# GpSimd's queue for the stores of staged weight sums, and a shorter lead for side work

## The chip, the cores and the metric

The kernel runs on one core of a Trainium2 chip. The metric is the device time of one execution in microseconds, the median of several runs. A core has a matrix engine (TensorE, PE in the profile), a vector engine (VectorE, DVE), a scalar engine (ScalarE, ACT), a general engine (GpSimd, POOL) and a sync engine (SyncE, SP) that here only issues transfers. Each engine has one queue of instructions and works through it in order. An instruction that waits for a semaphore holds everything behind it in its queue. SP, ACT and POOL can issue transfers; 16 DMA engines carry them out.

## The reference

All data is float32. For each of 4 batches there are 2048 tokens of width 512 and a context of 128 rows. The block does a gated cross attention and then a gated expert layer:

```python
Q = layernorm(x) @ Wq + bq;  K = ctx @ Wk + bk;  V = ctx @ Wv + bv
attn = softmax(Q @ K.T) / sqrt(512)
x = x + tanh(g_xattn) * (attn @ V)
z = layernorm(x)
e = argmax(z.mean(over tokens) @ Wr + br)          # one of 8 experts for a whole batch
h = relu(z @ W1[e] + b1[e])                        # 512 -> 2048
x = x + tanh(g_ffn) * (h @ W2[e] + b2[e])          # 2048 -> 512
```

Which expert a batch uses is known only once all its tokens have been through attention.

## The kernel before, in words

The two products of the expert layer are most of the arithmetic. The kernel computes them with Strassen's scheme in the Winograd form, which needs seven products of half-size blocks instead of eight, and for the first layer it does so on two levels. The price is sums and differences of blocks: of the weights, of the tokens z, and of the products. In the code a product is one of seven numbers, and `ORDER` gives their order.

The weights' sums are made once for each batch and half of the hidden width (`fh`), and this is called staging. `stage_half` loads a tile `base` with a part of W1 (`base_load`, line 593), forms sums in it and in a tile `tt` with `minus` (line 564), and stores both to the scratch arrays W1d in DRAM. It also loads a part of W2 into a tile named `base2` (`base2_load`, line 599), forms sums in place (`second_sums`) and stores that to W2d. Under the products GpSimd makes these sums. There is one buffer for `base` and one shared by `tt` and `base2`, so each load waits until the store of what lay there has landed. All stores go through `put` (line 584), which also tells the planner that the data will be there 9 us later. The first batch's weights are partly staged before the products begin, in tiles called `home` that are later used for other things.

The product loop takes weight tiles from a ring: four of one kind and two of the other. `fetch` issues the loads of these tiles on SP (lines 777, 784 and 790) as soon as a place is promised free, and an instruction on SP waits until TensorE has finished with the tile that lay there. `z_load` (line 888), the loads of y (957), the loads of xT (207) and the output stores (1137) are on SP too.

In a first-layer pass (`ffn1`) VectorE and GpSimd combine the seven products with running sums r and u. GpSimd makes those of lines 1000, 1006 and 1011. VectorE's line 1063 writes such a sum into the PSUM bank that the next product adds to, so TensorE waits for it. Second-layer passes (`ffn2`) have no work of that kind on GpSimd. There are 16 passes of each sort.

The order on every queue is written out by a planner in the kernel's own Python, at build time. It keeps a clock that a product loop advances (`tick`). Attention of later batches (the stream `slow`) and staging (`staged`) are generators that yield estimates of their steps' times; after each tick, `paced` lets them take steps, as their share allows and as long as the step's estimated start is no more than `SOON[0]` ahead of the clock (1.4 us before). `SOON` is also the size of a deliberate gap (`GAP`) after some steps of attention: after the power on GpSimd that gives rstd (line 220), after the exponentials, and after the copy of their transpose. Before the products begin, streams run by another rule, and the flag `ahead_of_ffn` tells the two apart.

The planner counts GpSimd's sums in `free["POOL"]`; a store takes no time there. `land` moves keys to the set `made` when the 9 us are over, and `fetch` only issues loads of weights that are in it.

Of the kernel before, what the change touches and what calls it, by code (L numbers as in the profile page):

```python
# [89 lines left out]
def flamingo(tc, ctx, x, xT, cxT, g_x, g_f, WqT, Wk, Wv, bqk, bv, Wr, br, W1, b1, W2, b2, out):  # L90
    nc = tc.nc
# [68 lines left out]

    zsum, Zs = {}, {}

    SOON = [1.4]
    MV = {}
    done_at, clock = {}, {"now": 0.0}
    ahead_of_ffn, fetched = [True], [0, 0]
# [9 lines left out]
    def room(ps):  # L176
        while held[ps] == ROOM[ps]:
            yield (("DMA", 0.3),)
        held[ps] += 1
# [16 lines left out]
    def attention(b, blk, pools):  # L196
# [13 lines left out]
        def statistics():  # L210
# [9 lines left out]
            nc.gpsimd.tensor_tensor(rstd, ve, mhalf, ALU.pow)  # L220
            yield ("DVE", 0.15), ("POOL", 1.05), ("GAP", 0.0 if ahead_of_ffn[0] else SOON[0])
            return mv, rstd
# [29 lines left out]
        for t in range(4):  # L252
# [4 lines left out]
            if t % 2:  # L257
                yield ("ACT", 1.2), ("GAP", SOON[0] * (t // 2) * (not ahead_of_ffn[0]))
        yield from room(ps_t)
# [9 lines left out]
        nc.vector.tensor_scalar(coef, coef, gx, None, ALU.mult)  # L269
        yield (("ACT", 0.6), ("GAP", SOON[0] * 0.8 * (not ahead_of_ffn[0]))), (("DVE", 0.4),)  # L270
        while MV[b][1] is None:
# [309 lines left out]
    made, landing = set(), []  # L581
    LAND = 9.0

    def put(dst, src, *keys):
        nc.sync.dma_start(dst, src)
        landing.append((clock["now"] + LAND, keys))

    def land(by):
# [14 lines left out]
    def second_sums(b, fh, kp, t, eng):  # L603

        b11, b21, b22, b12 = (t[:, i] for i in range(4))
        for o, l, r in ((b11, b12, b11), (b12, b22, b12), (b22, b22, b11), (b21, b21, b22)):
            yield minus(eng, o, l, r)
        put(
            W2d[b, fh][:, kp].rearrange("p o k c -> p o (k c)"), t,
            *((b, fh, "2") for _ in range(kp))  # L610
        )

    def first_half():
# [11 lines left out]
        def keep(place, n, pc, t):  # L625

            d, o = W1d[0, 0, place]
            put(d[:, o : o + n, pc], t, *((0, 0, place + j) for j in range(n * pc)))
# [53 lines left out]
    def stage_half(b, fh, eng, turns):  # L682
# [12 lines left out]
        def first_layer(pc, base):  # L695
            yield from inner_sums(eng, base)
            if pc and turns:
                yield (("DMA", 4),)
            tt = stp.tile([P, 3, 7, P], F32, tag="tt", name="tt")
            for i, took in enumerate(  # L700
                outer_sums(eng, *(t[:, i] for t, n in ((base, 4), (tt, 3)) for i in range(n)))
            ):
                yield took
                if i == 2:
                    put(W1d[b, fh, 4][0][:, :, pc], tt, *((b, fh, 4 + j) for j in range(3 * pc)))
            put(W1d[b, fh, 0][0][:, :, pc], base, *((b, fh, j) for j in range(4 * pc)))
# [620 lines left out]
    def paced(name, stream, more):  # L1327

        due[name] = min(due[name] + more, 1.0 + more)
        while stream and due[name] >= 1 and stream.at <= clock["now"] + SOON[0]:  # L1330
            due[name] -= 1
# [4 lines left out]
    def tick(dt, weight):  # L1336
# [5 lines left out]
        for s_ in list(loose):  # L1342
            while s_.at <= clock["now"] + SOON[0]:
                if not s_.step():
# [61 lines left out]
```

## Time and profile before

| | |
|---|---|
| median of 3 runs | 1742.46 us (1736.89 to 1744.96) |
| profiled execution, its own time | 1742.86 us |
| its span | 1741.1 us |
| TensorE busy, share of the span | 1686.3 us, 97% |
| VectorE, ScalarE, GpSimd busy | 1048.7, 581.9, 654.6 us |
| mean granted clock of TensorE | 0.989 of full speed |
| HBM traffic | 262.99 MB read, 117.44 MB written |

The page of a profile gives busy times, a row for each kind of instruction and for each kind of transfer. A wait is shown as who waited, at which line, for whom. SP's queue has waits of its own (SPq): they are no work, but they hold what stands behind. In a list by stretch of time, each pair of numbers is the busy time of an engine and its instructions in that stretch, and the granted clock of TensorE follows, as a share of full speed. Staging under the products lies at about 130 to 280, 420 to 635, 750 to 970 and 1080 to 1270 us.

### The profile page before, as it was taken

To read this page: it belongs to the slowest core of one execution; us is meant where nothing else is said; L and a number is where in the kernel's file an instruction comes from. 1 tells how busy PE (TensorE), PEld (TensorE's weight loads), DVE (VectorE), ACT (ScalarE), POOL (GpSimd) and SP (SyncE) were. 2 spreads that over 40 slices of the span, in tenths; PEclk is the share of its full clock that TensorE was granted. 3 is DMA by queue.
4 is the path that set the end of the run, shared out by engine and by line. 5 is a ranking of instruction groups with operands and counts; after the bars stand their busy time and mean duration, and the time that the engine had idled before them with its cause. 6 is when DMAs were issued, how large, how long until landed. Compare 5 with 4: busy or idle time off the path is not lost.

```text
span 1741.1 us, 21919 instructions
## 1 busy us (share of the span) xinstructions
PE 1686.3 (97%) x7965; PEld 1439.3 (83%) x7966; DVE 1048.7 (60%) x1663; ACT 581.9 (33%) x1284; POOL 654.6 (38%) x536
## 2 busy tenths in 40 slices
PE   6889999999999999998999999999999999999999
PEld 5667788888888888787878788888888888888887
DVE  5756576556666674757648565583846464746362
ACT  1524225253251614514144252322323242414150
POOL 0365424420648621366156520576514210331010
PEclk8989999999999999999999999999999999999999
DMA  7267777465687965478769564679744543545242
GB/s 296 97 255 287 280 259 287 157 237 190 247 324 259 356 235 178 156 284 299 288 244 344 193 229 142 228 276 318 292 150 155 164 160 101 180 145 174 91 136 80
DMA packets 143067, 381.87 MB, mean 219 GB/s; under 512 B 10480, under 2 KB 40176, under 8 KB 128624
## 3 DMA queue, kind: packets, MB, share of 16 engines
q1 hardware_dynamic: 136912, 342.43, 55.9%
q10 hardware_dynamic: 6048, 38.04, 5.5%
q8 instruction: 64, 1.05, 0.2%
q14 instruction: 43, 0.35, 0.1%
HBM read 262.99 MB, written 117.44 MB: 219 GB/s over the span
## 4 chain that ended last, share of the span: by engine, by line
PE 86%; DVE 6%; DMA 4%; issue 1%; ACT 1%; POOL 1%; SPq 0%; DVEq 0%; POOLq 0%; ACTq 0%
PE Y L811 34%; PE Q L811 23%; PE X L811 21%; DMA w<-W1d 3%; PE pav L288 2%; PE psc L234 2%; PE pt L335 1%; DVE st L214 1%; DMA home<-in_W_dram 1%; PE pm L417 1%; PE pv L450 1%; DVE x L276 1%; DVE c L1009 1%; PE pk L417 0%; DMA wq<-in_WqT_dram 0%
## 5 line engine op out<-in xcount | busy, mean ns | idle before, releaser
L811 PE MATMUL Y<-z,w 128*128 128x256 f32 x1296 | 322.8, 382 | 18.0 <-DMA w<-W1d 8.8
L811 PEld LDWEIGHTS Y<-z,w 128*128 128x128 f32 x1296 | 242.7, 190 | 65.2 <-DVE Q L1063 12.8
L978 ACT ACTIVATE h<-c,b1T 128x256 f32<-128x256 f32 x512 | 229.5, 500 | 86.8 <-DVE c L1009 37.1
L564 POOL TENSOR_TENSOR base<-base 128x512 f32<-128x512 f32 (+1 forms) x126 | 183.5, 1462 | 175.5 <-DMA base<-in_W_dram 171.2
L830 ACT COPY Y<-X 128x512 f32<-128x512 f32 x144 | 82.2, 571 | 467.6 <-PE X L811 467.2
L811 PE MATMUL Y<-w,h 128*128 128x256 f32 x1024 | 228.8, 380 | 0.0
L811 PE MATMUL X<-w,h 128*128 128x256 f32 x1024 | 227.9, 379 | 0.0
L811 PE MATMUL Q<-w,h 128*128 128x256 f32 x1024 | 226.9, 379 | 0.0
L811 PEld LDWEIGHTS X<-w,h 128*128 128x128 f32 x1024 | 193.9, 190 | 29.0 <-issue 3.1
L811 PEld LDWEIGHTS Y<-w,h 128*128 128x128 f32 x1024 | 194.7, 191 | 28.1 <-issue 2.0
L811 PEld LDWEIGHTS Q<-w,h 128*128 128x128 f32 x1024 | 194.3, 190 | 26.2
L811 PE MATMUL Q<-z,w 128*128 128x256 f32 x864 | 212.1, 385 | 1.3
L811 PE MATMUL X<-z,w 128*128 128x256 f32 x864 | 207.4, 379 | 0.0
L811 PEld LDWEIGHTS Q<-z,w 128*128 128x128 f32 x864 | 164.8, 193 | 28.6 <-issue 4.2
L1000 POOL TENSOR_TENSOR r<-r,cg 128x512 f32<-128x512 f32 x32 | 40.6, 1270 | 390.3 <-DVE cg L1081 388.4
L811 PEld LDWEIGHTS X<-z,w 128*128 128x128 f32 x864 | 163.5, 190 | 24.8 <-issue 3.3
L564 POOL TENSOR_TENSOR z<-z 128x256 f32<-128x256 f32 x156 | 129.0, 851 | 37.4 <-DVE z L564 33.6
L220 POOL TENSOR_TENSOR rstd<-ve,mhalf 128x4 f32<-128x4 f32 x32 | 34.9, 1089 | 279.1 <-DVE ve L219 279.0
L811 PE MATMUL Y<-w,s 128*128 128x256 f32 x512 | 113.6, 379 | 0.0
L1142 DVE SCALAR_TENSOR_TENSOR y<-Y,gf,y 128x512 f32<-128x512 f32 x64 | 47.8, 746 | 103.1 <-PE Y L811 101.9
L811 PEld LDWEIGHTS Y<-w,s 128*128 128x128 f32 x512 | 96.8, 190 | 12.9
L1142 DVE SCALAR_TENSOR_TENSOR y<-X,gf,y 128x512 f32<-128x512 f32 x32 | 23.9, 746 | 135.3 <-issue 70.7
(145 smaller groups left out, 2081.9 us busy)
## 6 DMA issues: line engine op xcount, KB each, us to landing
w<-W1d SPq DMA_DIRECT2D x108, 512.0 KB, 4.3
w<-W1d SPq DMA_DIRECT2D x108, 384.0 KB, 4.4
w<-W2d SPq DMA_DIRECT2D x64, 512.0 KB, 7.2
base<-in_W_dram SPq DMA_DIRECT2D x29, 1024.0 KB, 8.5
W1d<-base SPq DMA_DIRECT2D x14, 1792.0 KB, 9.3
w<-in_W_dram SPq DMA_DIRECT2D x48, 512.0 KB, 5.1
W1d<-tt SPq DMA_DIRECT2D x14, 1344.0 KB, 6.0
xT<-in_xT_dram SPq DMA_DIRECT2D x16, 1024.0 KB, 10.9
```

Of the source, the lines that this page charges most:

```text
L214: nc.vector.bn_stats(st, xt[:, t, :])
L220: nc.gpsimd.tensor_tensor(rstd, ve, mhalf, ALU.pow)
L234: nc.tensor.matmul(psc[:, t, :], lhsT=xTt[:, kc, t * P : (t + 1) * P], rhs=Mb[:, kc, :], start=kc == 0, stop=kc == KC - 1,)
L276: nc.vector.scalar_tensor_tensor(xt[:, t, :], t_, coef[:, t : t + 1], xt[:, t, :], ALU.mult, ALU.add)
L288: nc.tensor.matmul(pav[t][0], lhsT=pT[:, t * P : (t + 1) * P], rhs=Vb, start=True, stop=True)
L335: nc.tensor.transpose(pt[kc][0][:, t * P : (t + 1) * P], z[:, t, kc * P : (kc + 1) * P], ident)
L564: eng.tensor_tensor(o, l, r, ALU.subtract)
L811: nc.tensor.matmul(bank[:, c, :], lhsT=left(k, c), rhs=right(k, c), start=fresh and c == 0 and k == 0, stop=c == 1 and k == ks - 1, skip_g ...
L830: nc.scalar.copy(t["Y"], t["X"])
L978: nc.scalar.activation(h[ij][:, v, 2 * m + c, :], src[:, c, :], AF.Relu, bias=b1T[:, f + c : f + c + 1],)
L1000: eng.tensor_tensor(r[j], r[j], v, ALU.add)
L1142: nc.vector.scalar_tensor_tensor(o, v, gf, o, ALU.mult, ALU.add)
```

## The change

`put` issues its transfer on GpSimd's queue when the products have begun (`ahead_of_ffn` is then false), and on SP's queue before that, as it did. `SOON` becomes 0.8. Since the planner uses `SOON`, the order of attention and staging among the products changes on every queue, while the amount of work stays.

```diff
-    SOON = [1.4]
+    SOON = [0.8]
...
+    def staging_queue():
+        return nc.sync if ahead_of_ffn[0] else nc.gpsimd
+
     def put(dst, src, *keys):
-        nc.sync.dma_start(dst, src)
+        staging_queue().dma_start(dst, src)
         landing.append((clock["now"] + LAND, keys))
```

## The prediction

> **What bounds the kernel now.** I read the page first, for who is busy.
>
> ```profile
> span 1741.1 us, 21919 instructions
> PE 1686.3 (97%) x7965; PEld 1439.3 (83%) x7966; DVE 1048.7 (60%) x1663; ACT 581.9 (33%) x1284; POOL 654.6 (38%) x536
> w<-W1d SPq DMA_DIRECT2D x108, 384.0 KB, 4.4
> W1d<-base SPq DMA_DIRECT2D x14, 1792.0 KB, 9.3
> ```
>
> TensorE is busy 97% of the span, and the change neither adds nor removes a product, so a gain can only come out of its pauses. The two transfer rows matter later: a weight tile normally lands 4.4 us after its issue, a store of staged sums takes 9.3.
>
> Second, busy time by stretch (columns: start:end, length, then busy us and instructions of PE, PEld, DVE, ACT, POOL; granted clock, DMA share, GB/s). The cuts are where staging starts and stops.
>
> ```profile
> 130.00:280.00 150.00, 143.15 (x678) 121.83 (x677) 96.02 (x155) 56.96 (x128) 65.30 (x45) 0.98 0.74 274
> 280.00:420.00 140.00, 138.42 (x668) 117.36 (x667) 86.15 (x156) 54.74 (x125) 33.66 (x38) 1.00 0.56 198
> 420.00:635.00 215.00, 213.01 (x1027) 181.39 (x1026) 138.44 (x222) 73.73 (x168) 123.11 (x93) 1.00 0.82 298
> 750.00:970.00 220.00, 209.39 (x995) 177.48 (x994) 140.79 (x215) 73.37 (x167) 117.45 (x87) 0.99 0.77 283
> 1080.00:1270.00 190.00, 188.78 (x870) 164.29 (x869) 122.34 (x140) 57.10 (x116) 121.54 (x88) 1.00 0.77 269
> 1270.00:1730.00 460.00, 459.51 (x2124) 402.30 (x2123) 242.74 (x341) 143.61 (x290) 92.61 (x86) 1.00 0.43 140
> ```
>
> The four stretches with staging hold 6.9 + 2.0 + 10.6 + 1.2 = 20.7 us of TensorE's pauses; the 460 us without staging hold 0.5. Third, the list of waits says for what (total us, times, longest).
>
> ```profile
> PE Y L811 <- DMA w<-W1d: 8.8, 5, 3.6
> PE Y L811 <- DVE Q L1063: 7.4, 7, 2.8
> POOL base L564 <- DMA base<-in_W_dram: 171.2, 14, 27.6
> ```
>
> Fourth, the waits of SP's own queue from 130 to 1300 us.
>
> ```profile
> SPq L585 <- POOL base L564: 67.6, 21, 10.2
> SPq L585 <- POOL tt L564: 43.5, 11, 10.2
> SPq L585 <- POOL home L564: 11.0, 1, 11.0
> SPq L599 <- DMA W1d<-tt: 11.7, 7, 3.7
> SPq L593 <- DMA W1d<-base: 8.5, 4, 4.9
> ```
>
> SP, which must issue every weight tile in order, stands 122.1 us at the stores' line (585) until GpSimd has made the sums, and only 20.2 us at the later loads that reuse the stored tile. Fifth, the chain of waits shows what such a stop can cost (start, us, what), and two windows of 10 us give the clock.
>
> ```profile
> 163.73 1.74 POOL home L564
> 165.48 0.33 SPq L585
> ...
> 167.35 9.11 DMA w<-W1d
> ...
> 176.59 1.57 PE Y L811 x4
> ```
> ```profile
> 170.00:180.00 10.00, 6.43 (x25) 5.19 (x24) 5.05 (x8) 5.16 (x16) 9.77 (x6) 0.84 1.02 386
> 810.00:820.00 10.00, 7.78 (x28) 5.89 (x27) 8.34 (x15) 6.06 (x14) 8.80 (x6) 0.83 1.03 408
> ```
>
> The sum ends, the store leaves, only then two loads of y and a weight tile go out, all at once (386 GB/s); the tile takes 9.11 us instead of 4.4 and TensorE stood 3.57 us. After it the clock is 0.84 over 10 us: another 1.6 us.
>
> **The change, part by part.** It moves 45 of the 54 stores (14 of 1792 KB and one of 896 KB from base, 14 of 1344 KB from tt, 16 of 1024 KB into W2d) from SP's queue to POOL's; the nine issued before the products stay. It also lowers SOON from 1.4 to 0.8, which reorders attention and staging against the products. The profiled execution took 1742.86 us outside its span of 1741.1, beside the median of 1742.46, so the sum below is as good against either.
>
> *1. SP no longer stops at stores.* Behind them stand weight tiles (lines 777 to 790), y, xT and z loads. The stall at 173 to 176.6 us should go: y and the tile can be issued before 165, while the DMA is less loaded. Gain 3.57 + 1.6 = 5.2. The other weight waits are 8.8 - 3.6 = 5.2. One of 2.1 follows the two stores of 776.8 and 778.8 us: the tiles behind them left at 779.4 and took 9.9 us to land. I take that whole, and half of the remaining 3.1, since there base loads of 1 MB stand in front as well, which stay on SP: 2.1 + 1.6 = 3.7. Ends: 0 and 10.4 us for the two together; I take 8.9.
>
> *2. The new order.* In the program's order, between the first and last running sum that POOL makes of a first-layer pass (lines 1000, 1006, 1011), there stand 35 staging sums before the change and 10 after it, plus 6 stores. The first pass keeps its 4. These sums delay POOL's running sums and slow VectorE's own: line 1009 takes 0.69 us, up to 1.94 where POOL works beside it. VectorE's L1063 is then late and TensorE waits. Past the first pass that wait is 7.4 - 2.8 = 4.6 us, and the window at 810 adds 0.17 x 10 = 1.7 by its clock: 6.3. From 31 to 6 + 6 intruders, the loss falls by 19/31: gain 3.9 (ends 0 and 6.3).
>
> SOON itself removes no work. Every planner step comes up to 0.6 us later, so attention's last block ends after 2028 of 3360 product calls instead of 1834, and staging after 2520 instead of 2282. That costs nothing as long as the pieces keep ahead of their use: the last batch's first half is stored by call 2286 and used from 2520, the second half's first-layer sums by 2448 and used from 2730. If that lead were gone, the planner would issue staging in one piece with TensorE idle behind sums of some 5 us; the margin excludes it. TensorE's stalls on attention (pav on L276 3.1 us, with a clock of 0.95 after it) are dealt anew: 0, ends -4 and +8.
>
> *3. POOL pays.* No row shows a DMA issued by POOL. Lower end: SP's issue of the same stores, 0.33 to 0.56 us. Upper end: POOL held until the data landed, 7.5 us (median of these stores). I take 1.5: the smallest POOL instruction with its fixed cost (L220, 1.02 us) plus about SP's 0.5 for writing the pieces; it lies near the lower end because the work is the same as SP's. 45 x 1.5 = 68 us raise POOL from 655 to 722 us of 1741, still idle most of the time. It counts only where something waits for POOL: 8 stores stand directly ahead of a running sum and 7 ahead of rstd (L220), behind which VectorE's line 241 and all after it wait. SOON leaves 0.8 us of slack; of the remaining 0.7 us I let half reach TensorE (the PSUM banks cover some): 15 x 0.35 = 5.2. With 0.5 us for a store it is 0; with 5 us, 15 x 4.2 / 2 = 31. The store waits only for POOL's sums just before it, so the wait itself adds nothing to POOL's queue.
>
> *4. The wait that is next.* The loads at 593 and 599 need the store landed. SP reaches them sooner, since it is not held at 585, and the store leaves about 1 us later: the 20.2 us there will grow, I estimate to 40 to 60, and POOL's wait for base loads (171.2) with it. Weight tiles behind them were issued already or go out as late as now: 1 us (ends 0, 8).
>
> Sum: -5.2 - 3.7 - 3.9 + 5.2 + 1 = -6.6; 1742.9 - 6.6 = 1736 us.
>
> The Trainium skill, in "DMA: Bandwidth & Descriptors" (Issuing engines are not separate DMA queues), speaks against a gain: all issuers feed the same 16 engines, and another issuer saves only sequencer time. The measured 9.11 and 9.9 us against 4.4 include being queued behind other transfers, so the rule does not settle it; by it item 1's tiles would land as late as now, and the result would be near 1745. The same page's section Queues, rings and completion order has each engine alternate between queues by packets, which would let a tile pass a 1792 KB store; no run here shows it. The page puts the first byte of a DMA from GpSimd at about 1 us against 0.6, so a store would leave some 0.4 us later; by that price alone item 3 would cost 0.
>
> **Rivals.** *A, slower: POOL held by its stores.* If writing the pieces of a store (four rows per partition) takes GpSimd 4 us, item 3 is 15 x 3.2 / 2 = 24, and the result 1742.9 - 12.8 + 24 + 1 = 1755. It decides from the length at which 15 x (d - 0.8) / 2 eats 11.8 us: d = 2.4 us. For it: the base wait of 171.2 us shows that staging is tight, and POOL's queue is in order; against: POOL idles 62%. *B, all pauses go:* 10.4 + 6.3, pav's 4, nothing paid: about 1722. For it: 31 sums leave the first-layer passes; against: the DMA share is 1.02 in the stalled windows, whoever issues. *C, hidden anyway:* the tiles stay late because bandwidth is the limit, and POOL's cost cancels the new order's gain: 1742. *D, it does not do what it says:* excluded, the order shows 45 stores on POOL and no other change of work.
>
> **How the numbers follow.** Main forecast 0.47 (1736, own range 1728 to 1743, which is d from 0.5 to 2.4 us), A 0.30, B 0.13, C 0.10. The bound that a measurement can tell is 0.5%, 8.7 us, so 1733.8 and 1751.2. Faster: B and 0.23 of the main case, 0.36. Slower: A from d = 3.5 us on, 0.26. Same: the rest, 0.38. Range: from 1724, near B, to 1757, past A's 4 us.
>
> **What would show it.** SP's waits at 585 under the products gone and those at 593 and 599 at 40 to 60; TensorE's wait on w<-W1d under 3 us; its wait on L1063 near 5; POOL's stores at 1.5 us or less each. Wrong if POOL's stores take over 2.4 us, if VectorE's line 241 waits on rstd for many microseconds, or if tiles land as late as before.

## The result, and the profile after

The changed kernel takes 1758.16 us (1756.99 to 1763.36) beside 1742.93 us of the kernel before on the same chip: a ratio of 1.0101, interval 1.0079 to 1.0123. It is slower by 15 us; the forecast was 1736 (1724 to 1757). The profiled execution took 1757.94 us with a span of 1756.2. Lines from 585 on have moved by three: 793 is the line that was 790, 814 was 811, 939 was 936, 1066 was 1063.

The page of the kernel after, first the engines and then two of the transfers:

```profile
PE 1686.0 (96%) x7966; PEld 1438.4 (82%) x7966; DVE 1066.8 (61%) x1663; ACT 581.6 (33%) x1284; POOL 687.7 (39%) x581
...
w<-W1d SPq DMA_DIRECT2D x108, 384.0 KB, 4.4
...
W1d<-base POOLq DMA_DIRECT2D x14, 1792.0 KB, 8.7
```

TensorE's busy time has not changed (1686.3 before). Span less busy time was 54.8 us and is 70.2, so the whole loss, 15.4 us, is idle TensorE. The transfers' medians are about the same, and the stores are now POOL's. By stretch (start:end, length, busy us and instructions of PE, PEld, DVE, ACT, POOL; granted clock, DMA share, GB/s):

```profile
130.00:280.00 150.00, 137.28 (x635) 115.40 (x634) 98.83 (x148) 48.40 (x111) 62.56 (x47) 0.95 0.69 251
280.00:420.00 140.00, 134.93 (x659) 115.44 (x658) 81.64 (x141) 55.39 (x129) 42.13 (x44) 1.00 0.59 204
420.00:635.00 215.00, 208.05 (x976) 176.09 (x975) 144.95 (x218) 75.42 (x162) 121.41 (x97) 0.99 0.74 265
750.00:970.00 220.00, 208.15 (x994) 176.11 (x993) 136.69 (x223) 73.69 (x167) 101.29 (x77) 0.98 0.64 228
```

Beside the rows of before, TensorE is busy 5.9, 3.5, 5.0 and 1.2 us less. The two later stretches hold 187.58 us (1080 to 1270) and 459.27 us (1270 to 1730), 1.2 and 0.2 less, so nearly all was lost before 970 us. That is not the end of staging, whose last store leaves GpSimd at 1388.7 us in the changed kernel. Attention's last add (L276) is at 1132.6 us, 1050.7 before. What TensorE waited for, from 130 us on (total us, times, longest):

```profile
PE pav L288 <- DVE x L276: 15.0, 4, 6.6
PE pt L335 <- ACT x L322: 5.7, 10, 1.7
PE X L814 <- DMA w<-W1d: 4.5, 1, 4.5
PE Y L814 <- DMA w<-W1d: 4.3, 5, 2.0
PE Y L814 <- DVE c L1080: 4.1, 5, 1.4
PE pr L521 <- DVE zb L515: 2.5, 2, 2.2
PE Y L814 <- DVE Q L1066: 2.0, 5, 0.6
```

This list answers most of the question. The weight waits are 4.5 + 4.3 = 8.8 us, the same as before (8.8). The wait on L1066 fell from 7.4 to 2.0. The waits that belong to attention (pav, and pt, the transposes of its result), to the choice of the expert (pr) and to VectorE's sums c of a first-layer pass rose: pav from 3.7 to 15.0, pt from 2.9 to 5.7, c from 0.9 to 4.1, and pr is new with 2.5. That is +11.3 + 2.8 + 3.2 + 2.5 - 5.4 = +14.4 us, beside a loss of 15.4. Three rows of 2.4 us together are new and not shown, so the whole list rises by 16.8, a little more than the idle time.

SP's own waits from 130 to 1300 us:

```profile
SPq L793 <- DMA W1d<-base: 29.4, 4, 24.1
...
SPq L602 <- DMA W1d<-tt: 12.4, 3, 8.1
SPq L787 <- DMA W2d<-home: 9.8, 1, 9.8
SPq L787 <- DMA W2d<-base: 7.5, 1, 7.5
SPq L596 <- DMA W1d<-base: 7.2, 2, 4.6
```

The 122.1 us at the stores' line are gone. In their place SP now waits 46.7 us (29.4 + 9.8 + 7.5) at the lines that load weight tiles, 787 and 793, for staged weights that have not landed. Before, the same two lines waited 5.7 + 3.8 + 1.3 + 0.7 = 11.5 us for stores. The chain of work (start, us, what) shows two of the big stalls, one for attention and one for weights:

```profile
176.03 5.62 DVE h L939 x2
181.66 0.67 DVE x L276
...
182.37 3.70 PE pav L288 x4
...
224.86 8.97 DMA W1d<-base
233.83 0.02 SPq L793
...
233.90 4.01 DMA w<-W1d
...
237.95 2.08 PE X L814 x4
```

At 182 us TensorE had stood 6.4 us for one add of attention (L276, 0.67 us of work). That add stood in VectorE's queue behind two sums of 512 columns (L939) that took 5.62 us together. Such a sum alone takes 0.69 us. On GpSimd, two sums into tt ran from 173.34 to 177.97 us, then the store of tt from 178.26 to 179.00, then a sum of base from 178.93 to 181.10 (start, us, instruction):

```profile
173.34 4.63 POOL L564 TENSOR_TENSOR tt<-base,tt 128x896 f32<-128x896 f32 x2
178.26 0.74 POOL L588 DMA_DIRECT2D W1d<-tt  x1 [0.30 <-POOL tt L564]
178.93 2.17 POOL L564 TENSOR_TENSOR base<-base 128x896 f32<-128x896 f32 x1
```

The second stall, 4.5 us at 233.4, is of the other sort: a store leaves GpSimd at 224.86, and the weight tile that reads it could be issued only at 233.9. The third big one, at 954 to 960.5, is like the first: two VectorE sums of z (L564, 1.22 us each as a rule) took 5.99 us together beside GpSimd's sums into tt.

The row of one such VectorE sum, and the store's own row on GpSimd (duration in ns, least/median/most):

```profile
L939 DVE TENSOR_TENSOR h<-s,h x64: 658/691/3902, 192.4 to 1710.1; 128x512 f32<-128x512 f32 x64
```
```profile
L588 POOL DMA_DIRECT2D W1d<-base x12: 712/726/833, 181.4 to 1259.7; - x12
```

The store takes GpSimd 0.73 us. The same VectorE sum had a most of 1.76 us before, and has 3.90 now (the other kinds of h sums: up to 2.58 before, up to 3.23 now). The one of 3.90 is at 1351.6 us, behind the last add of attention; the second of the two at 176 us took 3.22.

The Trainium skill, in "SBUF — State Buffer" (SBUF: two separate sides), says that a VectorE operation with two SBUF inputs and a GpSimd operation that reads SBUF take turns: whichever starts first keeps the shared port pair for its whole instruction, and the other is blocked. Sums of up to 2.6 us agree with that: they start inside a GpSimd sum, wait for its rest and take their 0.69. So does one of 0.69 us at 1248.67 that starts 0.05 us ahead of a GpSimd sum; that sum takes 2.58 us instead of about 2.1.

Five h sums of 3.2 us and more in the changed kernel do not agree with it in one point. Each starts 0.14 to 0.18 us after a store has begun on GpSimd, about 0.5 us ahead of the sum of base behind the store, and yet ends only after that sum: the one at 178.43 ends at 181.65, the sum of base at 181.10. The store alone does not do it: at 639.19 a sum of h starts at the same place in a store (639.00 to 639.73), nothing follows on GpSimd, and it takes 0.68 us. With the stores on SP, in the kernel before and in soon_only_08 (below), no h sum takes over 2.58 us. Why a sum that has begun gives way there stays open.

### The profile page after: what moved, and what is told of

Its sections match the earlier page's. It is cut to its first block, busy times and chain, and to the rows that moved or that the text cites. A ratio compares the mean times of both kernels' runs of the same rounds, so it can differ in the third digit from the quotient of the medians.

```text
span 1756.2 us, 21928 instructions
## 1 busy us (share of the span) xinstructions
PE 1686.0 (96%) x7966; PEld 1438.4 (82%) x7966; DVE 1066.8 (61%) x1663; ACT 581.6 (33%) x1284; POOL 687.7 (39%) x581
## 4 chain that ended last, share of the span: by engine, by line
PE 81%; DVE 8%; DMA 6%; POOL 3%; ACT 1%; issue 1%; SPq 0%; DVEq 0%; POOLq 0%; ACTq 0%
PE Y L814 32%; PE Q L814 21%; PE X L814 21%; PE psc L234 2%; PE pav L288 2%; DMA w<-W1d 2%; POOL home L564 2%; DVE st L214 1%; PE pt L335 1%; DMA home<-in_W_dram 1%; DVE x L276 1%; DVE h L939 1%; DMA W2d<-home 1%; DMA base<-in_W_dram 1%; ACT x L322 1%
## 5 line engine op out<-in xcount | busy, mean ns | idle before, releaser
L814 PE MATMUL Y<-z,w 128*128 128x256 f32 x1296 | 323.8, 383 | 12.2 <-DMA w<-W1d 4.3
L564 POOL TENSOR_TENSOR base<-base 128x512 f32<-128x512 f32 (+1 forms) x126 | 180.4, 1436 | 164.0 <-DMA base<-in_W_dram 159.4
L564 POOL TENSOR_TENSOR z<-z 128x256 f32<-128x256 f32 x156 | 128.9, 849 | 40.3 <-DVE z L564 35.6
```

The lines of the kernel that those rows point to most:

```text
L564: eng.tensor_tensor(o, l, r, ALU.subtract)
L814: nc.tensor.matmul(bank[:, c, :], lhsT=left(k, c), rhs=right(k, c), start=fresh and c == 0 and k == 0, stop=c == 1 and k == ks - 1, skip_g ...
```

## The experiments

Three theories stood at the start. *Order*: the new order that SOON 0.8 makes puts GpSimd's sums beside VectorE work that TensorE needs soon. *Queue*: the stores on GpSimd cost by themselves. *Landing*: the staged data land too late for the loads that read them.

### One part at a time, and a middle value

The first run takes the new queue and leaves SOON at 1.4, so that the order on TensorE, VectorE and ScalarE is the one before. The second takes SOON alone. The other two are the same pair at 1.1.

```diff
 # queue_only_14: only this (queue_11: with SOON 1.1)
+    def staging_queue():
+        return nc.sync if ahead_of_ffn[0] else nc.gpsimd
...
-        nc.sync.dma_start(dst, src)
+        staging_queue().dma_start(dst, src)
```
```diff
 # soon_only_08: only this (sync_11: 1.1)
-    SOON = [1.4]
+    SOON = [0.8]
```

> Only the stores move to GpSimd's queue; SOON stays 1.4, so TensorE's, VectorE's and ScalarE's orders are those of before. Theory O (the new order of attention and staging under SOON 0.8 costs the 15 us, the queue does not): 1735 to 1743 us, TensorE's waits on L276 stay near 5 us, its waits on weight tiles fall from 8.8 us. Theory Q (the queue costs it: stores land later, and the loads that need them hold SP): 1752 to 1760 us, TensorE's waits on weight tiles above 12 us.

> Only SOON becomes 0.8; the stores stay on SP. Theory O: 1752 to 1765 us, with single waits of TensorE on VectorE's L276 of 5 to 7 us near 180 and 950 us, as after the change. Theory Q: 1740 to 1746 us.

> Stores on GpSimd's queue with SOON 1.1, beside the next run, which has the same order on the other engines with the stores on SP. Theory O: the pair lies together within 8 us, and off both 1743 and 1758 by what its own order gives, somewhere in 1735 to 1765. Theory Q: this one 10 to 18 us above the next.

> Stores on SP with SOON 1.1. Theory O: within 8 us of the run with the same order and the stores on GpSimd's queue. Theory Q: 1738 to 1748 us, 10 to 18 us below that run.

| run | stores on | SOON | us | ratio (interval) |
|---|---|---|---|---|
| queue_only_14 | GpSimd | 1.4 | 1751.68 | 1.0049 (1.0032 to 1.0067) |
| soon_only_08 | SP | 0.8 | 1764.32 | 1.0124 (1.01 to 1.0148) |
| queue_11 | GpSimd | 1.1 | 1756.07 | 1.0079 (1.0051 to 1.0107) |
| sync_11 | SP | 1.1 | 1769.64 | 1.0155 (1.0127 to 1.0183) |

None of the four runs fits its theories whole. queue_only_14 is near the time of theory Q, but with 7.5 us of weight waits, not over 12. soon_only_08 is in the range of theory O, with a wait of 6.1 us on L276 at 954 us, but near 180 us it waits for a weight tile instead. The pair at 1.1 lies 14 us apart with the queue the faster, which neither theory had.

Both parts lose alone, and they don't add: 8 us for the queue, 21 for SOON, 15 for both. At SOON 0.8 the queue makes the kernel 6 us faster, at 1.1 it makes it 14 us faster, at 1.4 it makes it 8 us slower.

With the stores on SP a shorter lead does just what the prediction's first step feared of SP. TensorE's waits in soon_only_08 and SP's, in two views:

```profile
PE Y L811 <- DMA w<-W1d: 16.8, 6, 7.4
...
PE X L811 <- DMA w<-W1d: 4.4, 1, 4.4
```
```profile
SPq L585 <- POOL tt L564: 42.9, 8, 12.4
SPq L585 <- POOL base L564: 36.6, 13, 5.5
```

SP stands at the store for up to 12.4 us in one piece, and TensorE has 21.2 us of weight waits (8.8 before, 36.7 in sync_11 with W2's 5.8). With the stores on GpSimd the weight waits are 8.8 at 0.8 and 12.2 at 1.1. So the queue does remove the waits that it was said to remove, when they are there; at SOON 1.4 only 8.8 us were, and it left 7.5.

The rest of SOON's loss is the same on either queue: soon_only_08 has 5.7 us on pt, 4.2 on c and 2.5 on pr, and the changed kernel 5.7, 4.1 and 2.5. pav rises with either part and most with both: 3.7 us before, 7.7 with the queue alone, 8.2 with SOON alone, 15.0 with both. VectorE is busy with all 256 h sums for 213.9 us before, 211.5 with SOON alone, 219.5 with the queue alone and 233.1 with both.

What it costs at an unchanged order is seen in queue_only_14, first by TensorE's waits and then on VectorE (start, us, instruction):

```profile
PE Y L814 <- DVE Q L1066: 10.7, 9, 3.8
PE pav L288 <- DVE x L276: 7.7, 3, 4.6
PE Y L814 <- DMA w<-W1d: 7.5, 5, 2.5
PE Y L814 <- ACT Q L1068: 4.0, 1, 4.0
```
```profile
177.18 4.61 DVE L939 TENSOR_TENSOR h<-h,h 128x512 f32<-128x512 f32 x2
...
182.31 2.37 DVE L555 TENSOR_SCALAR b2g<-b2g,gf 128x512 f32<-128x512 f32 x1
184.60 1.40 DVE L276 SCALAR_TENSOR_TENSOR x<-pav,coef,x 128x512 f32<-128x512 f32 x2
```

The stall at 173 to 176.6, the first gain of the prediction, is gone: its weight tile left at 161.59 instead of 167.35. TensorE then goes on, reaches attention's next product at 180.8 (its start at 185.39 less the longest wait of 4.6), and stands there for L276. In the kernel before it stood 3.6 us for the tile, and meanwhile GpSimd finished its sums; the same two VectorE sums took 1.29 us, at 181.39. The early stall had covered the later one. Removing it moved it.

### Where the store is put, and how it is cut

late_sp_14 leaves the stores on SP and the order as before, but puts each store 4 us of the planner's clock later into SP's queue, so that SP waits less for the sum; the planner counts the data as landed those 4 us later too. split_14 is queue_only_14 with each store as two halves of 64 partitions.

```diff
 late_sp_14:
+            late.append((clock["now"] + DELAY, dst, src, keys))    # DELAY = 4.0
...
+            nc.sync.dma_start(dst, src)                            # once that time is reached
 split_14:
+            for r in (slice(0, P // 2), slice(P // 2, P)):
+                nc.gpsimd.dma_start(dst[r], src[r])
```

> The order of before (SOON 1.4) with the stores on SP, but each store is put into SP's queue 4 us of the planner's clock later, when GpSimd's sums are nearly done. Theory S (SP's stop at the stores is what weight tiles are late for): SP's waits at the stores fall from 122 us to under 60, TensorE's waits on weight tiles from 8.8 us to under 5, 1732 to 1739 us. Theory N (the tuned order hides the stop): 1740 to 1748 us.

> The stores on GpSimd's queue with SOON 1.4, each store issued as two halves of 64 partitions, so that GpSimd has 45 more instructions of some 0.6 us and the same bytes. Theory V (a store instruction on GpSimd holds VectorE's sums, and this is the 8 us by which the queue alone is slower than before): 5 to 12 us above the queue alone, 1757 to 1764 us. Theory O (only the fall of the order matters): 1748 to 1755 us.

late_sp_14: 1752.84 us, 1.0062 (1.0047 to 1.0077). SP's stops at the stores fell to about 66 us, but the loads that reuse the tiles then waited 50.7 us (26.1 for tt, 24.6 for base) instead of 20.2. Nearly halving SP's stops without GpSimd's queue gains nothing either; the time is above both theories' ranges.

split_14: 1798.60 us, 1.0327 (1.0313 to 1.0341), the largest effect of all, and far above what either theory had. A half takes GpSimd 0.55 to 0.63 us, so two cost some 0.5 us more than a whole; 45 times that is 22 us of an engine that is idle more than half of the time. But the halves landed later, and SP waited for them. The page's transfer row, then two of SP's waits:

```profile
W1d<-base POOLq DMA_DIRECT2D x28, 896.0 KB, 12.2
```
```profile
SPq L606 <- DMA W1d<-tt: 56.0, 9, 19.3
SPq L600 <- DMA W1d<-base: 34.4, 6, 8.1
```

A whole store of base took 9.0 us to land in queue_only_14, a half 12.2; SP's waits at the two reloads are 90.4 us against 53.7 there, and TensorE's weight waits 38.5 against 7.5. So the time to land is a strong lever: SP now waits for it in order, ahead of every weight tile.

### Lead and gap apart

SOON is used twice by the planner: how far ahead a step may start, and how long a gap it leaves after some steps of attention. Both runs have the stores on GpSimd.

```diff
+    SOON, GAPS = [0.8], [1.4]     # lead08_gap14; [1.4], [0.8] in lead14_gap08
...
-            ("GAP", 0.0 if ahead_of_ffn[0] else SOON[0])
+            ("GAP", 0.0 if ahead_of_ffn[0] else GAPS[0])
```

> The changed kernel with the two uses of SOON parted: lead 0.8, gaps in attention 1.4. If the shorter gaps place attention's sums badly: near 1750 us. If the shorter lead does: near 1758 us. If any reordering gives its own time: anywhere from 1745 to 1765 us.

> Stores on GpSimd's queue, lead 1.4, gaps 0.8. If the shorter gaps place attention's sums badly: near 1758 us. If the shorter lead does: near 1751 us. If any reordering gives its own time: anywhere from 1745 to 1765 us.

1765.45 us (1.0131, 1.0114 to 1.0148) and 1766.97 us (1.0146, 1.013 to 1.0163): both worse than either pure setting with this queue (1758 and 1752). The first has 27.0 us of waits on one kind of weight tile, 18.1 of them at once; the second has 12.6 us on L1066 and 7.2 on pav. So neither lead nor gap alone is the cause: each costs more than both together, and TensorE waits at other places.

### Without GpSimd's long sums

```diff
+    def staged_sum(eng, o, l, r, fresh):
+        if ahead_of_ffn[0]:
+            return minus(eng, o, l, r)
+        if fresh:
+            eng.memset(o, 0.0)
+        else:
+            minus(eng, *(t[..., 0:1] for t in (o, l, r)))
```

This cuts the staging sums under the products and leaves order, stores and loads as they are: the planner is told the sum's full time. A fill of 128x896 still takes GpSimd 0.8 us where the sum took about 2.1. It was made at both values of SOON and on both queues.

> The kernel before with GpSimd's staging sums under the products cut to little: sums into fresh places become a fill with zeros, sums in place touch one column, so the staged weights are not the right ones; loads, stores, queues and the order stay. Theory C (what the order costs is GpSimd's sums, which come late and slow VectorE's sums beside them): 1718 to 1735 us, and the changed kernel cut alike within 5 us of it. Theory D (attention's place among the products costs by itself): this one 10 us or more below the next.

> The changed kernel with the same sums cut to little (the staged weights are not the right ones). Theory C: 1718 to 1735 us, TensorE's waits on L276 under 4 us. Theory D: TensorE's waits on L276 stay near 15 us, the time 10 us or more above the kernel before cut alike.

> Stores on GpSimd's queue at SOON 1.4, with GpSimd's staging sums under the products cut: sums into fresh places are a zero fill, sums in place one column wide, so the result is not the reference's. Beside 1732.0 us of the stores on SP with the same cut. Theory S (the queue costs by what GpSimd's long sums and the stores do to VectorE together): without the sums the queue costs nothing, 1728 to 1736 us. Theory Q (the queue costs by itself, by late landings that hold ScalarE's x load and SP's reloads): 1737 to 1744 us, with TensorE's wait on ScalarE at 4 us or more.

> Stores on SP's queue at SOON 0.8, GpSimd's staging sums under the products cut in the same way (not the reference's result). With whole sums SOON 0.8 cost 21 us with the stores on SP. Theory S (the shorter lead costs because SP waits for long sums before each store and weight tiles stand behind it): with the sums cut SP has little to wait for, 1730 to 1740 us, weight waits under 8 us. Theory T (the order itself costs, by weight tiles issued late whatever the sums take): 1745 to 1760 us, weight waits still over 12 us.

| | stores on SP | stores on GpSimd |
|---|---|---|
| SOON 1.4, whole sums | 1743 | 1752 |
| SOON 1.4, sums cut | 1732 (0.9948, 0.9929 to 0.9967) | 1746 (1.001, 0.9996 to 1.0024) |
| SOON 0.8, whole sums | 1764 | 1758 |
| SOON 0.8, sums cut | 1743 (0.9997, 0.9983 to 1.0011) | 1740 (0.9983, 0.997 to 0.9996) |

The sums' part in the loss is clear for attention: with them cut, the changed kernel's wait on pav falls from 15.0 to 1.0 us, and the slowest h sum from 3.90 to 1.24. But cutting them brings the kernel before 11 us too, and 7.5 us stay between the two kernels, more than theory C allowed and less than D's 10. What TensorE waits for in small_sums_after shows what the cut leaves:

```profile
PE Y L823 <- ACT Q L1077: 9.3, 1, 9.3
PE pt L335 <- ACT x L322: 5.8, 10, 1.7
...
PE Y L823 <- DVE c L1089: 4.1, 5, 1.4
PE pr L521 <- DVE zb L515: 3.9, 2, 2.2
```

pt, c and pr wait as long as with whole sums, so they come with the order itself. The 9.3 us for ScalarE are new: the changed kernel has 0.2 there, and small_sums_before 1.7. So the 7.5 us are not a measure of what the order costs by itself. With the stores on SP that disturbance is 1.7 us at most, and the measure is better: with the sums cut SOON 0.8 costs 11 us (1743 beside 1732), pt, c and pr rise by 10.6 together (3.2 to 13.8), and the weight waits are 9.4 us beside 9.6. With whole sums SOON cost 21 us there, 12.4 of them weight waits. So theory S of small_soon_08 is right that the weight waits come from SP's stops for long sums, though they are not under 8; its time was missed, since the order's own 11 us stay, and theory T's was missed too.

For the queue theory S, that it costs only through the sums, falls: at SOON 1.4 with the sums cut the queue costs 14 us, more than with them, and TensorE waits 9.1 us on ScalarE, as theory Q had it (its range ended at 1744). The chain of small_queue_14 shows the place:

```profile
130.57 10.27 DMA b2g<-in_b_dram
...
140.85 0.02 ACTq L205
```

ScalarE's queue stands at its next load of x (L205) until a transfer of SP's (b2g) has landed, 10.3 us after its issue; the copies of Q behind it are late, and TensorE waits those 9.1 us. In queue_only_14, with whole sums, they are 4.0. In the kernel before that wait is not in the list, and with the sums cut it is 1.7 us. Two staged stores leave GpSimd at 129.3 and 130.1 us, both ahead of b2g; in small_sums_before, on SP, one of them stood ahead of b2g (130.4, b2g 131.8) and the other behind it (132.9). Why ScalarE's load waits for b2g at all was not examined.

A second place is at 583 to 612 us. The same stretch in small_queue_14 and in small_sums_before, by queue (packets, MB, share of 16 engines; q1 is SP's, q0 GpSimd's) and by transfer (median us to landing):

```profile
DMA packets 2535, 10.86 MB, mean 374 GB/s; under 512 B 185, under 2 KB 697, under 8 KB 1883
...
q1 hardware_dynamic: 1621, 4.48, 41.5%
q0 software_dynamic: 624, 4.26, 38.3%
...
w<-in_W_dram SPq DMA_DIRECT2D x2, 512.0 KB, 19.3
w<-W2d SPq DMA_DIRECT2D x2, 512.0 KB, 22.2
```
```profile
DMA packets 3117, 10.99 MB, mean 379 GB/s; under 512 B 208, under 2 KB 720, under 8 KB 2427
...
q1 hardware_dynamic: 2827, 8.87, 80.9%
...
w<-W2d SPq DMA_DIRECT2D x3, 512.0 KB, 11.4
...
w<-in_W_dram SPq DMA_DIRECT2D x2, 512.0 KB, 9.9
```

The bytes and the rate are the same. On SP's one queue the stores of tt and base were issued at 597.3 and 597.9, behind four weight tiles (590.5 to 596.8). On their own queue they were issued at 594.9 and 596.2, also behind the first three of these tiles, but over the stretch the two queues share the engines about half and half (the store at 583.2, of W2d, counted in), and the tiles take twice as long. TensorE stood 3.8 us for one of them. Here one queue in order had been a priority: what was issued first was served first.

With whole sums the same is seen in the slowest weight tile of all: 13.2 us from issue to landing in the kernel before, 21.3 in queue_only_14 (medians 5.3 and 5.4). In the changed kernel it is 13.7, so this is no part of its loss.

The Trainium skill, in "DMA: Bandwidth & Descriptors" (Queues, rings and completion order), has each engine take turns between its queues packet by packet. The shares of 41.5 and 38.3% agree with it. The prediction used that rule for a tile that would pass a store; here it worked the other way, and let stores pass tiles.

### The store instruction by itself

aside_store_14 keeps the real stores on SP, at SOON 1.4, and adds 45 small ones on GpSimd that nobody waits for.

```diff
+        if not ahead_of_ffn[0]:
+            nc.gpsimd.dma_start(aside[turn[0] % 8], ident)
+            turn[0] += 1
```

> The kernel before (stores on SP's queue, SOON 1.4, same order on every engine) with one more small store behind each staged store under the products: 128 x 128 of the identity to a DRAM place that nobody reads, issued by GpSimd, 45 in all. No staged data changes its queue or its landing. Theory V (the store instruction on GpSimd holds what VectorE does beside it): a good part of the +8.5 us of the queue alone at SOON 1.4 appears, 1747 to 1755 us, and VectorE's slowest hsum sums (L936) pass 3 us as they do with the queue alone. Theory L (the queue's loss comes from when the staged data lands and from what goes out earlier on SP): 1740 to 1746 us, slowest hsum near 2.6 us.

1748.11 us, 1.0029 (1.0013 to 1.0045), between the two theories. The instruction takes 0.56 us, 45 of them 25 us of GpSimd, and the kernel loses 4.7 us. Weight waits rise by 5.1 us to 13.9 and the wait on VectorE's Q by 3.1 to 10.5; the slowest h sum is 2.76 us, not over 3. So some of the 8 us of the queue may be GpSimd's time, but not through slower VectorE sums, as theory V had it. The 64 KB that each small store moves are in this number too, and that late and slow landings have the rest is not shown.

### Other leads

```diff
 # sync_13, sync_15, sync_16, sync_20: only SOON; queue_16: with the stores on GpSimd
-    SOON = [1.4]
+    SOON = [1.3]     # 1.5, 1.6, 2.0
```

> Stores on SP as before, SOON 1.3. Theory T (1.4 is a point that was picked, and neighbouring orders are slower whichever way SOON moves): 1750 to 1770 us. Theory M (a longer lead is better and a shorter one worse): 1744 to 1752 us, between 1.4 and 1.1.

> Stores on SP as before, SOON 1.5. Theory T: 1750 to 1770 us. Theory M: 1735 to 1743 us.

> The changed kernel with SOON 1.6 in place of 0.8: stores on GpSimd's queue, a longer lead. Theory M (a longer lead is better on either queue, as 1.1, 1.3, 1.4, 1.5 were with the stores on SP): 1735 to 1748 us. Theory T (every order has its own collisions, no trend with the stores on GpSimd: 1758 at 0.8, 1756 at 1.1, 1752 at 1.4): 1748 to 1765 us.

> The kernel before with SOON 1.6 in place of 1.4, stores on SP's queue. With the stores on SP the times so far are 1764 us at 0.8, 1770 at 1.1, 1758 at 1.3, 1743 at 1.4, 1744 at 1.5, and TensorE's weight waits 21.2, 36.7 (with W2's), 23.5, 8.8, 13.6 us. Theory M (a longer lead takes the weight waits away, until they are gone): 1734 to 1746 us, weight waits under 14 us. Theory T (each order has its own collisions; 1.4 is a good draw): 1746 to 1765 us.

> The kernel before with SOON 2.0 in place of 1.4, stores on SP's queue. Theory M (a longer lead is better on SP's queue): 1730 to 1746 us, and if so the best version with the whole work. Theory T (each order has its own collisions): 1746 to 1765 us, with waits on attention's adds (L276) or on VectorE's L1063 in place of weight waits.

| SOON | 0.8 | 1.1 | 1.3 | 1.4 | 1.5 | 1.6 | 2.0 |
|---|---|---|---|---|---|---|---|
| stores on SP, us | 1764 | 1770 | 1758 | 1743 | 1744 | 1749 | 1743 |
| stores on GpSimd, us | 1758 | 1756 | | 1752 | | 1756 | |

The ratios of the new ones are 1.0086 (1.0056 to 1.0116) at 1.3, 1.0016 (1.0003 to 1.0029) at 1.5, 1.0031 (1.0018 to 1.0044) at 1.6, 1.0003 (0.9989 to 1.0017) at 2.0, and 1.0068 (1.0046 to 1.009) for queue_16. With the stores on SP a lead under 1.4 loses 15 to 27 us by these ratios, and a longer one gains nothing. Neither theory holds throughout: the runs at 1.3 and 1.6 lie in theory T's ranges, 2.0 in M's, and 1.5 between them. With the stores on GpSimd the four times lie within 6.5 us and show no trend, as theory T had it. No version with the whole work beats the kernel before.

## Why the prediction was wrong, step by step

*Step 1, SP no longer stops at stores: gain 8.9.* The stops went, as forecast, and so did the stall at 173 us. The gain did not come: weight waits are 8.8 us in both. With the order unchanged they fell by 1.3 us only. A tile that arrives earlier lets TensorE reach the next late thing earlier; the stall at 173 had hidden one of 4.6 us at L276, which my list of waits before could not show. The step asked what is late next on SP, not on VectorE.

*Step 2, the new order: gain 3.9, SOON costs nothing, attention dealt anew at 0. This is the step that failed.* Its first half was right: with fewer sums inside the first-layer passes, the wait on L1066 fell by 5.4 us (7.4 to 2.0), more than forecast. But the sums that left those passes went somewhere, and I counted intruders only in one place. At the two largest stalls, 182 and 960 us, they stand beside VectorE's h and z sums, behind which attention's add at L276 waits: pav rose by 11.3 us, beyond the bound of +8 (it was 3.7 us before; the 3.1 of the prediction is the longest wait alone). pt and pr rose by 5.3 together on top of it, and c by 3.2, which had no term; these three stay with the sums cut. "That costs nothing" was argued from the pieces' lead over their use, and no row backed it: SOON alone, with the stores on SP, costs 21 us, 11 with the sums cut. Its other large part, +12.4 us of weight waits where SP stands at stores for long sums, is what GpSimd's queue takes away. The two parts of the change were also priced one by one, while pav rises by 4.0 and 4.5 with one of them and by 11.3 with both, and the h sums by 5.6 and -2.4 with one and by 19.2 with both.

*Step 3, POOL pays 5.2.* The duration was too high: 0.73 us, not 1.5, beside a fixed 0.30 us ahead of it, and POOL's busy time rose by 33 us, not 68. The fifteen places that I counted show no loss in the changed kernel: VectorE's line 241 waits 0.3 us on rstd (1.5 before), and L1066 costs less than before. What the stores do is another thing: an h sum that starts inside one waits out the staging sum behind it too (3.2 us instead of 2.6). The term is near what aside_store_14 lost, 4.7 us, but that is luck: there it came with weight tiles (+5.1) and the Q wait (+3.1).

*Step 4, the next wait: 1 us.* The reloads at 596 and 602 hold SP about as long as before (7.2 and 12.4 us beside 8.5 and 11.7), not the 40 to 60 us that I had estimated. The growth, from 11.5 to 46.7 us, is at the weight tiles' own loads, 787 and 793. Either part alone raises it less: to 20.2 us with the queue, to 17.7 with SOON. One of 24.1 us cost TensorE 4.5. POOL's wait for base loads, which was to grow, fell from 171.2 to 159.4. The place and the price were both missed, and the priority that one queue gives to what is issued first was not thought of.

*The rivals.* A gave 1755, close to the time, but its condition was a store of 2.4 us or more, and the store takes 0.73: the time was nearly met by a mechanism that did not happen. C (tiles as late as before) is true of the weight waits' sum, 8.8 and 8.8, but they are not the same waits.

What stays open: how the queue's 8 us at SOON 1.4 divide between GpSimd's time, slower tiles and the load of x behind b2g, why pav rises by more with both parts than by the two alone, and why one order has fewer collisions than its neighbour. The runs show the kinds of collision, not a rule that would forecast the sum.

## What to carry to other kernels

When a tuned order is dealt anew, count the collisions of the moved work in every place where it can land, not just in the place that it leaves; a term "dealt anew, 0" deserves the widest range of the sum. Before you credit the removal of a stall, look at what it was hiding: here the next engine needed those microseconds. And a single in-order queue is also a priority, so before you move bulk stores to a queue of their own, look which small urgent loads were ahead of them in line.

## What the hardware showed that was not expected

- A VectorE sum of two 128x512 f32 tiles in SBUF takes 0.69 us alone, up to 2.6 beside GpSimd's staging sums, and 3.2 to 3.9 where it starts inside a store on GpSimd that a staging sum follows at once. Inside a store that nothing follows it takes 0.68. A sum of 1024 columns went from 1.22 us to about 3.
- A DMA of 128 partitions issued by GpSimd takes it 0.54 to 0.83 us, 0.73 for most stores into W1d, and starts 0.30 us after the sum that it waits for. Cut into two halves of 64 partitions, each takes 0.55 to 0.63, and the landing of the 1792 KB piece's halves takes 12.2 us instead of 9.0.
- With bulk stores on a second queue, 512 KB weight tiles took 19 to 22 us to land instead of 10 to 11, at the same total rate (374 and 379 GB/s).
